# Edge tables copied in two halves, in pieces, inside the first pass of a graph network kernel

## The chip, the cores and the metric

The kernel runs on one core of a Trainium2 chip. The metric is device time in microseconds (us) of one execution; less is better. Five engines work beside each other, each with its own queue of instructions served in order: PE (matrix products), DVE (vector work), ACT (activation functions, and here a queue that issues DMA), POOL (here: indirect DMA, that is gathers and scatters), SP (here: a queue that issues DMA). Sixteen DMA engines move the data of all queues.

## What is computed

Four graph layers on one graph of N = 6250 nodes with D = 16 features and E = 200000 edges; after each the layer's result is added to x and normalized per node. The edges' inputs are `src`, `dst`, `edge_weight`, `edge_weight1` and `edge_attr_16`.

```python
edge_index = jnp.stack([src, dst])
x = _layernorm(x + _L0_gnn_ref(x, edge_weight, src, dst), axis=-1)        # segment_sum(tanh(x[src] * edge_weight), dst)
x = _layernorm(x + _L1_gnn_ref(x, edge_attr_16, W_msg, b_msg, W_attn, b_attn, src, dst), axis=-1)
x = _layernorm(x + _L2_gnn_ref(x, edge_weight1, W, b, src, dst), axis=-1)  # segment_max(x[src] * edge_weight1, dst) @ W.T + b
x = _layernorm(x + _L3_gnn_ref(x, edge_index, ...), axis=-1)               # two GIN convolutions with segment_sum(x[src], dst)
```

Layer 1 makes two 16 x 16 matrices per edge from its 16 features (`efeat @ W_msg + b_msg`, `efeat @ W_attn + b_attn`), multiplies both with the features of the source node, takes a softmax of the second over the edges of each target node and sums the first with it. The inputs given here have their edges sorted by `dst`.

## The kernel before

Edge p * 1600 + j lies in partition p (of 125) at column j (of J = 1600). The kernel needs edges in order of their targets.

**The start.** SP loads x, dst (`load_dst`) and src. DVE compares neighbouring targets (L274, L275), PE adds up the 125 partitions' answers, and `unordered` (L280) is the number of partitions in which an edge goes backwards, read into a register on every engine. DVE and PE then make the keys of the first 120 columns (`keys_first`, L265: `keys_made`, `keys_turned`, `keys_kept`), SP writes them to `key_d` (L252) and reads two blocks back, spread over 125 partitions (`load_keys`, L262, into `keys0`). ACT waits for the first of them (the copy to `arrived`, L285) and issues three copies from DRAM to DRAM (L287): edge weights to `ew_d` and `ew1_d` (0.8 MB each) and edge features to `ef_d` (12.8 MB). L289 is the branch around `sort_edges`: where `unordered` is above 0, the edges are sorted, and every input of the edges is scattered to its place (the list `given`, L199), over what the copies wrote. With the given inputs the branch is not taken; the engines meet at its end.

**The first pass** (`edge_scan("l0", ...)`) goes over eight batches of 200 columns. For 80 columns of each, POOL gathers the rows of x (L97, one gather a column, tile `xb`, two buffers). For the other 120, DVE makes one-hot matrices from a block of keys (`one_hot`, L469; SP asks for keys two blocks ahead), PE multiplies them with the table of x (L499, `select`), and DVE picks and sums (L503, L508). In the batch that follows, the message is formed (`tanh_message`: DVE times `ew` at L912, ACT's tanh at L914) and DVE scans it along the edges (L533). The order on each engine is that in which the program is written (`tc.manual_schedule`).

**Beside the first pass** runs a list of jobs (`prelude`): `at(k, ...)` puts a job before the k-th of 240 selects. Among them are the keys of later batches, the ends of the nodes' edges (51 gathers on POOL, `in_run`), the table of chunks for layer 1 (50 scatters on POOL, `chunk_d`), the load of `ew` from `ew_d` (k = 20), and `edge_rows`: 64 times 25 columns of `ef_d` are loaded by SP (`er_ef`, L681, by way of `store`, L93 and L94), split by ACT and DVE into three bf16 parts and written by SP to `edges_d`. The first of these loads is job 14.

**The later passes.** Layer 1 gathers chunks of `edges_d`, layer 2 repeats the scan with `ew1` (loaded at L1315 from `ew1_d`), layer 3 scans twice without weights.

Of the kernel before, what the change touches and what calls it, by code (L numbers as in the profile page):

```python
# [8 lines left out]
F32 = mybir.dt.float32  # L9
BF16 = mybir.dt.bfloat16  # L10
I32 = mybir.dt.int32
U16 = mybir.dt.uint16
# [8 lines left out]
P = 125  # L21
# [26 lines left out]
def tile_gnn_resnorm(ctx: ExitStack, tc: tile.TileContext, a: dict, out: bass.AP):  # L48
# [42 lines left out]
    def store(eng, to, of):  # L91

        eng.dma_start(to[:112], of[:112])  # L93
        eng.dma_start(to[112:], of[112:])  # L94
# [50 lines left out]


    src_d = dram.tile([E, 1], I32, name="src_d")
    dst_d = dram.tile([E, 1], I32, name="dst_d")
    ew_d = dram.tile([E, 1], F32, name="ew_d")
    ew1_d = dram.tile([E, 1], F32, name="ew1_d")  # L150
    ef_d = dram.tile([E, D], F32, name="ef_d")
    given = [(src_d, a["src"].unsqueeze(1)), (dst_d, a["dst"].unsqueeze(1)), (ew_d, a["edge_weight"].unsqueeze(1)),
# [4 lines left out]
    def sort_edges(sp, pp, dst):  # L157
# [6 lines left out]
        with tc.For_i(0, E, P) as e0:  # L164
# [33 lines left out]
            for t, (to, of) in zip(rows, given):  # L198
                nc.gpsimd.indirect_dma_start(  # L199
                    out=to, out_offset=bass.IndirectOffsetOnAxis(ap=at, axis=0), in_=t, in_offset=None)  # L200

# [55 lines left out]

    def load_keys(ep, k, keys=None):

        if keys is None:  # L260
            keys = ep.tile([P, BW], U16, name="keys", bufs=2)
        nc.sync.dma_start(keys, key_d[k * BC * P:k * BC * P + BW].partition_broadcast(P))  # L262
        return keys

    def keys_first(first):  # L265

        with tc.tile_pool(name="keys0p", bufs=1, space=PSUM) as pp:
            keys_kept(kp, 0, keys_turned(lambda r, c: pp.tile([128, 512], F32, name="scratch")[:r, :c], keys_made(kp, 0)))
        return [load_keys(kp, k, to) for k, to in enumerate(first)]

    with tc.tile_pool(name="sort", bufs=1) as sp, tc.tile_pool(name="sortp", bufs=1, space=PSUM) as pp:
        back = sp.tile([P, J], F32, name="backwards")
        worst = sp.tile([P, 1], F32, name="worst")
        nc.vector.tensor_tensor(back, dst[:, 1:J + 1], dst[:, :J], op=OP.is_lt)  # L274
        nc.vector.tensor_reduce(worst, back, AX.X, OP.max)  # L275
        n_ps = pp.tile([1, 1], F32, name="n_ps")
        nc.tensor.matmul(n_ps, worst, ones, start=True, stop=True)
        n_back = sp.tile([1, 1], I32, name="n_back")
        nc.vector.tensor_copy(n_back, n_ps)
        unordered = nc.values_load(n_back, min_val=0, max_val=P)  # L280
        keys0 = keys_first([None, None])
        arrived = consts.tile([1, 1], F32, name="arrived")
        with tc.manual_schedule():

            nc.scalar.copy(arrived, keys0[0][:1, :1])  # L285
            for to, of in given[2:]:
                nc.scalar.dma_start(to.rearrange("(p j) f -> p (j f)", p=1600),  # L287
                                    of.rearrange("(p j) f -> p (j f)", p=1600))
        with tc.If(unordered > 0):  # L289
            sort_edges(sp, pp, dst)  # L290
            nc.sync.dma_start(src, src_d.rearrange("(p j) o -> p (j o)", j=J))
            load_dst(dst, dst_d.rearrange("e o -> (e o)"))
            keys_first(keys0)

# [176 lines left out]

    def edge_scan(tag, table, parts, F, message, pen, tmp, beside=None, first=None, keys=None):

# [9 lines left out]
        with tc.tile_pool(name=f"es_{tag}", bufs=3) as ep, \  # L483
# [56 lines left out]

            keys = list(keys or [load_keys(ep, k) for k in range(0 if first is None else 1, 2)])
            ohs = one_hot(ep, keys.pop(0)) if first is None else first
# [135 lines left out]
    def edge_rows_load(e, c):  # L678
        if c < J:
            e.ef[c] = e.tmp.tile([P, WE, D], F32, name="er_ef", bufs=2)  # L680
            store(nc.sync, e.ef[c], ef_d.rearrange("(p j) f -> p j f", j=J)[:, c:c + WE, :])  # L681

# [233 lines left out]
    def prelude(kp):  # L916
# [6 lines left out]
        def at(k, do):  # L923
            jobs.setdefault(k, []).append(do)
# [13 lines left out]
        def put(**what):  # L938
            for k, f in what.items():
                now[k] = f  # L940
# [7 lines left out]
        for b in range(1, NB):  # L948
            k = 5 + 20 * (b - 1)
            at(k, lambda b=b: put(lo=keys_made(kp, b)))  # L950
            at(k + 3, lambda: put(kT=keys_turned(scratch, now["lo"])))
            at(k + 4, lambda b=b: keys_kept(kp, b, now["kT"]))
        at(12, lambda: put(e=ends_begin(now["sp"])))
        for i, j0 in enumerate(range(0, NJ1, NS)):
# [25 lines left out]
        for i in range(3):  # L980
            at(180 + 4 * i, lambda i=i: node_weights(i))
        at(20, lambda: store(nc.sync, ew, ew_d.rearrange("(p j) o -> p (j o)", j=J)))
        at(14, lambda: put(r=edge_rows_begin(now["rp"])))
# [8 lines left out]

    rows, carry = edge_scan("l0", a["x"], parts, D, tanh_message, None, lp0, prelude(kp), keys=keys0)
    x1 = node.tile([P, NJ, D], F32, name="x1")
# [316 lines left out]
    with tc.tile_pool(name="l2", bufs=1) as lp:  # L1311
        pen = lp.tile([P, J], F32, name="pen")
        nc.vector.tensor_scalar(pen, keep, -1.0, BIG, op0=OP.add, op1=OP.mult)
        ew1 = lp.tile([P, J], F32, name="ew1")
        nc.sync.dma_start(ew1, ew1_d.rearrange("(p j) o -> p (j o)", j=J))  # L1315

# [123 lines left out]
```

## Time and profile before

| | us |
|---|---|
| median of 3 runs | 7642.45 (7641.83 to 7643.04) |
| the profiled execution | 7640.91 |
| its span | 7639.1 |
| PE busy | 6793.4 (89%) |
| DVE busy | 6769.3 (89%) |
| POOL busy | 5894.5 (77%) |
| ACT busy | 1915.9 (25%) |
| first one-hot of the first pass (DVE L469) | starts at 74.77 |
| first gather of the first pass (POOL L97) | starts at 75.73 |
| first gather of layer 1 (POOL, tile `g`) | starts at 1279.74 |
| load of `ew1` for layer 2 (SP L1315) | issued at 4256.2 |

How to read it: times in the profile count from the start of the span. L12 is line 12 of the kernel before. Busy times of the engines overlap, so they don't add up to the span. A row names engine, line, operation, and the tile written <- the tiles read. What stands in brackets is the idle time of the engine ahead of the row and what ended it.

### The profile page before, as it was taken

To read this page: it belongs to the slowest core of one execution; us is meant where nothing else is said; L and a number is where in the kernel's file an instruction comes from. 1 tells how busy PE (TensorE), PEld (TensorE's weight loads), DVE (VectorE), ACT (ScalarE), POOL (GpSimd) and SP (SyncE) were. 2 spreads that over 40 slices of the span, in tenths; PEclk is the share of its full clock that TensorE was granted. 3 is DMA by queue.
4 is the path that set the end of the run, shared out by engine and by line. 5 is a ranking of instruction groups with operands and counts; after the bars stand their busy time and mean duration, and the time that the engine had idled before them with its cause. 6 is when DMAs were issued, how large, how long until landed. Compare 5 with 4: busy or idle time off the path is not lost. (4 is left out here: it accounts for less than half of the span.)

```text
span 7639.1 us, 133337 instructions
## 1 busy us (share of the span) xinstructions
PE 6793.4 (89%) x55586; PEld 5218.5 (68%) x55586; DVE 6769.3 (89%) x7933; ACT 1915.9 (25%) x3214; POOL 5894.5 (77%) x4906
## 2 busy tenths in 40 slices
PE   5888795799999999999999499999499998799995
PEld 5888795344444444444444299999499998799995
DVE  6999895899999999999999788999488887688885
ACT  0122120455555555555555400000000000000000
POOL 5888887777777777777777588888688887788886
PEclk9999897899999999999999799999699999899997
DMA  4344442122222222222222422222122222122221
GB/s 125 90 115 100 113 107 75 43 50 52 53 50 53 50 52 53 49 53 50 52 53 50 135 46 45 56 45 50 33 45 52 49 55 48 29 48 54 54 48 33
DMA packets 288155, 460.45 MB, mean 60 GB/s; under 512 B 135318, under 2 KB 187902, under 8 KB 283240
## 3 DMA queue, kind: packets, MB, share of 16 engines
q1 hardware_dynamic: 121160, 331.29, 12.9%
q0 software_dynamic: 166032, 106.01, 12.9%
q10 hardware_dynamic: 336, 14.40, 0.6%
q8 instruction: 442, 7.24, 0.4%
q14 instruction: 185, 1.52, 0.1%
HBM read 256.61 MB, written 206.15 MB: 61 GB/s over the span
## 5 line engine op out<-in xcount | busy, mean ns | idle before, releaser
L499 PE MATMUL all_ps<-parts,oh 125*128 125x208 bf16 (+1 forms) x46080 | 4004.1, 251 | 217.9 <-DVE kept L503 98.7
L499 PEld LDWEIGHTS <-oh 125*128 125x128 bf16 x46080 | 3985.5, 98 | 236.7 <-issue 130.1
L97 POOL DMA_INDIRECT hg<-table_x,g x1760 | 2061.5, 1171 | 545.1 <-issue 543.2
L97 POOL DMA_INDIRECT xb<-table_x,src x1280 | 1616.4, 1263 | 424.5 <-issue 423.6
L1101 PE MATMUL la<-e,ident 128*128 128x512 f32 x3520 | 1560.6, 596 | 4.5 <-DVE e L1088 3.8
L508 DVE TENSOR_REDUCE xb<-kept 125x64 f32<-125x832 f32 x960 | 1509.9, 1573 | 33.1
L503 DVE TENSOR_TENSOR kept<-all_ps,place 125x832 f32<-125x832 f32 x960 | 974.7, 1015 | 330.5 <-PE all_ps L499 322.6
L1101 PEld LDWEIGHTS la<-e,ident 128*128 128x128 f32 x3520 | 652.2, 190 | 743.9 <-issue 737.7
L97 POOL DMA_INDIRECT xb<-in_x,src x640 | 833.5, 1302 | 266.6 <-issue 193.3
L1053 DVE TENSOR_TENSOR e<-mm,hg 128x1024 f32<-128x1024 f32 x880 | 1013.4, 1210 | 10.6 <-DMA hg<-table_x,g 10.5
L97 POOL DMA_INDIRECT xb<-table_l3b,src x640 | 797.2, 1246 | 208.7 <-issue 208.7
L1048 PE MATMUL mm<-w_h,eT 98*128 98x512 bf16 x1760 | 668.1, 380 | 237.5 <-DVE e L1053 167.5
L469 DVE TENSOR_SCALAR oh<-keys,mykey 125x1504 bf16<-125x1504 uint16 x1272 | 792.8, 684 | 78.0 <-SPq L289 55.5
L1065 ACT ACTIVATE e<-e,epen 128x256 f32<-128x256 f32 x1760 | 797.6, 501 | 112.1 <-DVE e L1053 110.5
L1081 ACT ACTIVATE e<-e 128x1024 f32<-128x1024 f32 x440 | 465.1, 1057 | 1001.8 <-DVE e L1079 984.6
L1049 PE MATMUL mm<-w_l,eT 98*128 98x512 bf16 x1760 | 669.4, 380 | 0.0
L1049 PEld LDWEIGHTS <-eT 98*128 98x128 bf16 x1760 | 169.7, 96 | 637.5 <-issue 533.3
L1079 DVE TENSOR_TENSOR e<-e,st 128x1024 f32<-128x1024 f32 x440 | 519.4, 1221 | 7.6
L1088 DVE TENSOR_TENSOR e<-e 128x1024 f32<-128x1024 f32 x440 | 516.4, 1214 | 0.0
L1048 PEld LDWEIGHTS <-eT 98*128 98x128 bf16 x1760 | 170.8, 97 | 238.6 <-issue 57.1
L461 ACT ACTIVATE ln_s<-ln_s,eps_t 125x35 f32<-125x35 f32 (+1 forms) x8 | 2.5, 315 | 1176.2 <-DVE ln_s L460 1176.2
L97 POOL DMA_INDIRECT g<-edges_d,eidx x220 | 208.0, 946 | 83.7 <-PE la L1102 64.9
(366 smaller groups left out, 3457.4 us busy)
## 6 DMA issues: line engine op xcount, KB each, us to landing
keys<-key_d SPq DMA_DIRECT2D x318, 367.2 KB
rows_l<-st SPq DMA_DIRECT2D x220, 384.0 KB
edges_d<-er_t SPq DMA_DIRECT2D x64, 546.9 KB
hg<-table_x,g POOLq DMA_INDIRECT x1760, 2.6
rows_l<-sc SPq DMA_DIRECT2D x16, 1400.0 KB
xb<-table_x,src POOLq DMA_INDIRECT x1280, 2.8
ef_d<-in_edge_attr ACTq DMA_DIRECT2D x1, 12500.0 KB
er_ef<-ef_d SPq DMA_DIRECT2D x64, 175.0 KB
```

What stands on the lines that cost most here:

```text
L97: nc.gpsimd.indirect_dma_start(out=dst_ap, out_offset=None, in_=table, in_offset=bass.IndirectOffsetOnAxis(ap=idx, axis=0))
L469: nc.vector.tensor_scalar(oh[:, g, :], keys, mykey[:, g:g + 1], None, op0=OP.is_equal)
L499: nc.tensor.matmul(o, oh[:, g, (c + i) * P:(c + i) * P + 128], parts[:, q, a0:a0 + n, :].rearrange("p a f -> p (a f)"), start=(g == 0 and ...
L503: nc.vector.tensor_tensor(kept.rearrange("p (h i) a f -> p h (i a) f", i=2), all_ps[:P, :, :2 * W].rearrange("p h (i f) -> p h i f", f=F), ...
L508: nc.vector.tensor_reduce(xb[:, j:j + SG, :], kept.rearrange("p i a f -> p i f a"), AX.X, OP.add)
L1048: nc.tensor.matmul(ps[:, i, :], eT[:, s + i, :], w_h, start=True, stop=False)
L1049: nc.tensor.matmul(ps[:, i, :], eT[:, s + i, :], w_l, start=False, stop=True)
L1053: nc.vector.tensor_tensor(e[:, s:s + 2, :].rearrange("p s (i x) -> p (s i) x", x=2 * D), ps.rearrange("p s (i x) -> p (s i) x", x=2 * D), ...
L1065: nc.scalar.activation(part(e, 0)[:, k], part(e, 0)[:, k], AF.Identity, bias=epen[:, t, k:k + 1])
L1079: nc.vector.tensor_tensor(sc, sc, top.rearrange("p (i o) -> p i o", o=D).unsqueeze(1).to_broadcast([128, 4, D, D]), op=OP.subtract)
L1088: nc.vector.tensor_tensor(part(e, 1)[:, s:s + 4], part(e, 1)[:, s:s + 4], part(e, 0)[:, s:s + 4], op=OP.mult)
L1101: nc.tensor.matmul(ps, ident, e[:, s, :], start=(s == 0), stop=False)
```

## The change

The tables `ew_d`, `ew1_d` and `ef_d` get two halves of E rows. `sort_edges` scatters to the first; the inputs as they came are copied to the second. A new register `half` on SP holds E where no edge goes backwards and 0 otherwise, and every load from the three tables starts at that row (`by_target`). The copies are taken out of the place ahead of the branch and written as jobs 1 to 10 of the first pass: one each for the weights, eight for the features, of 25000 edges (1.6 MB) each, all issued by ACT. The copy to `arrived` is gone. Keys are no longer read ahead of the branch; `edge_scan` reads its first two blocks itself.

```diff
-    ew_d = dram.tile([E, 1], F32, name="ew_d")
-    ew1_d = dram.tile([E, 1], F32, name="ew1_d")
-    ef_d = dram.tile([E, D], F32, name="ef_d")
+    ew_d = dram.tile([2 * E, 1], F32, name="ew_d")
+    ew1_d = dram.tile([2 * E, 1], F32, name="ew1_d")
+    ef_d = dram.tile([2 * E, D], F32, name="ef_d")
...
-                    out=to, out_offset=bass.IndirectOffsetOnAxis(ap=at, axis=0), in_=t, in_offset=None)
+                    out=to[:E, :], out_offset=bass.IndirectOffsetOnAxis(ap=at, axis=0), in_=t, in_offset=None)
...
-    def load_keys(ep, k, keys=None):
-
-        if keys is None:
-            keys = ep.tile([P, BW], U16, name="keys", bufs=2)
+    def load_keys(ep, k):
+
+        keys = ep.tile([P, BW], U16, name="keys", bufs=2)
         nc.sync.dma_start(keys, key_d[k * BC * P:k * BC * P + BW].partition_broadcast(P))
         return keys
 
-    def keys_first(first):
-
+    def keys_first():
         with tc.tile_pool(name="keys0p", bufs=1, space=PSUM) as pp:
             keys_kept(kp, 0, keys_turned(lambda r, c: pp.tile([128, 512], F32, name="scratch")[:r, :c], keys_made(kp, 0)))
-        return [load_keys(kp, k, to) for k, to in enumerate(first)]
...
         unordered = nc.values_load(n_back, min_val=0, max_val=P)
-        keys0 = keys_first([None, None])
-        arrived = consts.tile([1, 1], F32, name="arrived")
-        with tc.manual_schedule():
-
-            nc.scalar.copy(arrived, keys0[0][:1, :1])
-            for to, of in given[2:]:
-                nc.scalar.dma_start(to.rearrange("(p j) f -> p (j f)", p=1600),
-                                    of.rearrange("(p j) f -> p (j f)", p=1600))
+        came = sp.tile([1, 1], I32, name="came")
+        nc.vector.tensor_scalar(came, n_ps, 0.0, float(E), op0=OP.is_equal, op1=OP.mult)
+        half = nc.values_load(came, engines=(mybir.EngineType.SP,), min_val=0, max_val=E)
+        keys_first()
         with tc.If(unordered > 0):
             sort_edges(sp, pp, dst)
             nc.sync.dma_start(src, src_d.rearrange("(p j) o -> p (j o)", j=J))
             load_dst(dst, dst_d.rearrange("e o -> (e o)"))
-            keys_first(keys0)
+            keys_first()
+
+    def by_target(t):
+        return t[bass.ds(half, E), :]
...
-            keys = list(keys or [load_keys(ep, k) for k in range(0 if first is None else 1, 2)])
+            keys = [load_keys(ep, k) for k in range(0 if first is None else 1, 2)]
...
-            store(nc.sync, e.ef[c], ef_d.rearrange("(p j) f -> p j f", j=J)[:, c:c + WE, :])
+            store(nc.sync, e.ef[c], by_target(ef_d).rearrange("(p j) f -> p j f", j=J)[:, c:c + WE, :])
...
+        for i, (to, of) in enumerate(given[2:4]):
+            at(1 + i, lambda to=to, of=of: nc.scalar.dma_start(to[E:, :].rearrange("(p j) o -> p (j o)", p=80),
+                                                               of.rearrange("(p j) o -> p (j o)", p=80)))
+        for i in range(8):
+            at(3 + i, lambda i=i: nc.scalar.dma_start(
+                ef_d[E + i * E // 8:E + (i + 1) * E // 8, :].rearrange("(p j) f -> p (j f)", p=100),
+                a["edge_attr_16"][i * E // 8:(i + 1) * E // 8, :].rearrange("(p j) f -> p (j f)", p=100)))
...
-        at(20, lambda: store(nc.sync, ew, ew_d.rearrange("(p j) o -> p (j o)", j=J)))
+        at(20, lambda: store(nc.sync, ew, by_target(ew_d).rearrange("(p j) o -> p (j o)", j=J)))
...
-    rows, carry = edge_scan("l0", a["x"], parts, D, tanh_message, None, lp0, prelude(kp), keys=keys0)
+    rows, carry = edge_scan("l0", a["x"], parts, D, tanh_message, None, lp0, prelude(kp))
...
-        nc.sync.dma_start(ew1, ew1_d.rearrange("(p j) o -> p (j o)", j=J))
+        nc.sync.dma_start(ew1, by_target(ew1_d).rearrange("(p j) o -> p (j o)", j=J))
```

In the order of instructions that the built program has on ACT, the copies of both weights and the first four pieces of the features stand ahead of the branch, and four pieces behind it; SP's way past the branch waits for all eight hardware DMA semaphores, as before.

More of the change, by code (lines that the diff above doesn't have):

```diff
@@ L470, in one_hot, with edge_scan @@
         return oh
-    def edge_scan(tag, table, parts, F, message, pen, tmp, beside=None, first=None, keys=None):
+    def edge_scan(tag, table, parts, F, message, pen, tmp, beside=None, first=None):
         is_max = pen is not None
```

## The prediction

> **What bounds the kernel now.** I read the page's slices first, since the change touches the start: is time lost there?
>
> ```profile
> span 7639.1 us, 133337 instructions
> ...
> DVE  6999895899999999999999788999488887688885
> ...
> POOL 5888887777777777777777588888688887788886
> ```
>
> The first slice of 191 us is busy to 5 or 6 tenths, the next ones to 8 or 9. The stretches of the start and the order of time say why:
>
> ```profile
> 10.00:20.00 10.00, 0.62 (x3) 0.26 (x3) 8.52 (x24) 0.00 (x0) 0.00 (x0) 1.00 0.02 5
> ...
> 30.00:70.00 40.00, 0.00 (x0) 0.00 (x0) 0.00 (x0) 0.00 (x0) 0.00 (x0) 1.00 0.98 322
> ```
>
> ```profile
> 19.32 0.37 SPq L252 DMA_DIRECT2D key_d<-kT  x1
> 21.72 53.84 SPq L262 DMA_DIRECT2D keys<-key_d  x3
> 27.68 0.19 ACT L285 CAST arrived<-keys 1x1 f32<-1x1 uint16 x1 [25.64 <-SPq L289]
> 27.69 1.23 ACTq L287 DMA_DIRECT2D ew_d<-in_edge_weight  x2
> 28.96 0.60 ACTq L287 DMA_DIRECT2D ef_d<-in_edge_attr  x1
> 74.77 4.62 DVE L469 TENSOR_SCALAR oh<-keys,mykey 125x1504 bf16<-125x1504 uint16 x8 [55.48 <-SPq L289]
> ...
> 75.73 1.56 POOL L97 DMA_INDIRECT xb<-in_x,src  x1 [71.83 <-SPq L289]
> ```
>
> From 30 to 70 us no engine works (the columns are PE, its weight loads, DVE, ACT, POOL, clock, DMA share, GB/s) and the DMA engines are 98% busy at 322 GB/s with the three copies of L287, 14.4 MB. Everything waits at L289, the branch around the sort. Its own row shows how:
>
> ```profile
> L289 SPq EVENT_SEMAPHORE  x8: 17/17/17, 23.5 to 74.6; - x8
> ```
>
> SP passes the branch by waiting for all eight hardware DMA semaphores, the copies' among them, and the last comes at 74.6. POOL starts 1.1 us behind it.
>
> What sets the end of the pass that follows (75 to 1279 us) I took from the waits of that stretch (total, times, longest) and the pass's last steps:
>
> ```profile
> POOL xb L97 <- issue: 193.3, 634, 0.3
> ...
> DVE xb L912 <- DMA xb<-in_x,src: 39.2, 2, 19.7
> ```
>
> ```profile
> 1239.78 0.96 DVE L912 TENSOR_TENSOR xb<-xb,ew 125x768 f32<-125x768 f32 x1
> ...
> 1264.67 1.49 DVE L912 TENSOR_TENSOR xb<-xb,ew 125x1280 f32<-125x1280 f32 x1 [19.54 <-DMA xb<-in_x,src]
> ...
> 1279.74 0.97 POOL L97 DMA_INDIRECT g<-edges_d,eidx  x1 [16.89 <-DVE carried L610]
> ```
>
> POOL never waits for anything but its own 0.3 us of issue: 640 gathers of x, 51 of runs and 50 scatters of chunks in one unbroken row, from 75.73 on. DVE twice stands still for them, 19.66 us at 855 to 874 and 19.54 us at the end. So the first pass is a gather chain of 1264.67 - 75.73 = 1188.9 us from POOL's start, and DVE has 39.2 us to spare. The three later passes start behind it and are not touched.
>
> **The change, part by part.** The sum is made against the profiled execution, 7640.9 us with 7639.1 of span; the median of the runs is 7642.45, 1.5 more.
>
> 1. *Where the copies go.* The diff writes them into the first pass, but nothing on ACT holds them there. In the order of instructions of the built program, six of ACT's ten copies (ew, ew1 and four of the eight ef pieces: 0.8 + 0.8 + 4 x 1.6 = 8.0 MB) stand ahead of the branch, at ACT's very start; four pieces (6.4 MB) follow it. SP still waits for all eight DMA semaphores at the branch. So the wait is not removed; it gets shorter and starts earlier.
>
> 2. *When the branch is passed.* Copies: 288 packets of 50 kB, 18 for each of the 16 DMA engines, took from 29.5 (1.8 us after the first issue) to 74.6, 2.51 us each. 8.0 MB are 10 for each: 25.1 us. They now share the engines with x, dst and src (2.0 MB): 125 rows each, whose packets took 0.178, 0.35 and 0.40 us, 116 us in all or 7.2 for each engine. First data at 2.4 (first issue at 0.76 as SP's today, plus 1.6). Earliest end 2.4 + 25.1 + 7.2 = 34.7. ACT's second, third and fourth piece wait for semaphores of earlier transfers (x, dst, the first piece), so I add 2 us for gaps: 36.7. The compute ahead of the branch must end by then too: src landed by 12.5, the keys' 6.8 us ended at 19.3, key_d was there at 21.7. If src is 10 us late behind copies, that ends at 32, still covered; if it comes with the last of the copies, key_d ends the wait (rival B). POOL starts 1.1 later: 37.8 instead of 75.73, **37.9 us earlier**. Bounds: a packet alone on an idle engine took 1.85 us, so 2.4 + 18.5 + 7.2 = 28.1 and POOL 46.5 earlier; with src last, 45 and 29.6 earlier.
>
> 3. *The last 6.4 MB beside the pass.* 8 packets for each engine, 8 x 2.51 = 20 us from the branch on. A gather of x lands 3.2 us after its issue and POOL issues one each 1.51 us with eight in flight, so it can take 12 us before POOL waits. Bounds: 0, as at 1282 to 1300, where 7.3 MB of zeros kept the DMA engines full at 399 GB/s and the gathers kept their 1.25 us step; and, were every gather held until the copies are done, 20 + 3 - 8 x 1.5 = 11 us. The zeros went in packets of 3008 bytes, these have 50 kB; the row is near in load, not in packet size. I take **3 us lost**.
>
> 4. *Keys.* keys0 was read ahead of the branch and is now read behind it: issue to arrival 5.8 us (21.72 to 27.5), up to 20 more beside the copies. DVE and PE thus start 6 to 26 us behind POOL instead of 1 ahead. Cost 0, hidden by DVE's 39.2 us of waiting for gathers. POOL depends on DVE with room enough: ck_at is written at 589.1 and used at 668.4, the scans that free a batch's buffer end at 1070 for gathers at 1133.8, the last group of five in run_i at 328.8 for gathers from about 401. The nearest room is 64 us. Beyond 39 us each us of lateness would cost one.
>
> 5. *Small things.* One DVE comparison (0.15 us, as L279) and one more register load on SP, ahead of 7 us of key work that is covered. One or two register instructions before each of the 131 loads through `half`: SP's 128 er_ef issues take 0.3 to 0.4 us each and SP is idle most of the time; keys are asked for two batches (29 us) ahead. ew1 is loaded at 4256 and used at 4513. The 1.28 us table load of ACT moves to the first er_t copy, where ACT waits anyway. Together 0.
>
> 6. *The new wait on SP.* The first er_ef load now waits for all ef pieces, with the next keys queued behind it. It stands 51 us after DVE's start (74.8 to 125.9); the copies end some 20 to 30 us after the branch. Cost 0.
>
> Sum: -37.9 + 3 = **-35 us**; profiled 7606, and with the 1.5 to the median **7607**.
>
> **Rivals.**
>
> *A, more gain.* The copies overlap with the inputs better than added times say, with packets at 1.85 us and no gather delayed: 7642.45 - 46.5 = 7596. For it: the inputs ran at 248 GB/s, below the copies' 322. Against: no stretch of the copies was faster than 344 GB/s.
>
> *B, the inputs wait in line.* src is issued behind 50 kB packets and arrives with the last of them at 34.7; then 6.8 us of keys, 2.4 for key_d and one for issue: branch at 45, POOL at 46, 29.6 us earlier, and gathers lose 3 to 8: 7616 to 7621. For it: where the copies met the second keys load (the trace's packet records, about 30 us), five engines began their first copy only once the keys' packets were through, served as they came. Against: at most half of the copies are issued before src is, since ACT waits for x, dst and its own first piece.
> By the Trainium skill, "DMA: Bandwidth & Descriptors", section "Queues, rings and completion order", a DMA engine takes turns between the queues that have work, a packet each: then src is not last, and the sum stays 7607, where service in order of arrival gives B's 7616 to 7621. In the few packets seen, the trace does not agree with it.
>
> *C, little or nothing.* B, and gathers held for the full 11 us, and the instruction fetches at the branch behind copies as well (PE's took 3.9 us on idle DMA engines; five times that is 16 more): gain 29.6 - 11 - 16 = 3, 7640.
>
> *D, slower.* Step 6 goes wrong: SP stands at er_ef, keys run out. It decides once copies last longer than 51 us, plus 29 of keys in hand, plus DVE's 39, plus the 35 won: 154 us after DVE's start, 6.4 MB at 42 GB/s. At 200 us: 7688. Against it: DMA engines 25% busy in that stretch and 322 GB/s before.
>
> **How the numbers follow.** Forecast 0.55 (7600 to 7614 by itself), A 0.12, B 0.20, C 0.08, D 0.05. The predicted time is 7607. The range 7596 to 7622 takes in the bounds of step 2, B, and leaves out C and D. About 0.2% (15 us, 7627) is what measuring can tell from no change: faster is forecast, A and B, 0.87; same is C, 0.08; slower D, 0.05.
>
> **What would show it.** Right: ACT's first DMA issue at about 0.8; SP's last wait at the branch at 35 to 38; POOL's first gather near 38; DVE's first one-hot 6 to 26 us later; then again an unbroken POOL row, the last gather's wait on DVE still there at the end, and g's first gather near 1245; the later passes as long as before. Wrong: a branch past 42 (B), gaps over 0.3 us between POOL's first 30 gathers (step 3), no wait of DVE for gathers at the pass's end (then DVE, not POOL, sets it and step 4 failed), or SP held at er_ef (D).

## The result and the profile after

The changed kernel takes 7593.25 us (median of 5 runs, 7588.63 to 7595.56) against 7642.45; the ratio is 0.9935, with a 95% interval of 0.9921 to 0.995. The profiled execution took 7588.63 us with a span of 7586.8, which is 52.3 less than before. The forecast was 35 less. Where the 52.3 us lie, from first instructions of the stages in both traces:

| stage | before | after | difference |
|---|---|---|---|
| to POOL's first gather | 75.73 | 36.25 | -39.5 |
| first pass, to the first gather of `g` | 1204.0 | 1203.9 | -0.1 |
| layer 1, to the gather of `fx` | 2976.7 | 2975.6 | -1.1 |
| tail of layer 1, from `fx` to the store of `table_x` | 84.2 | 73.8 | **-10.4** |
| layer 2, from there to DVE's step on `carried` | 1048.3 | 1046.7 | -1.6 |
| layer 3 to the end | 2250.1 | 2250.6 | +0.5 |

First the page's slices after:

```profile
span 7586.8 us, 133608 instructions
...
DVE  7999994999999999999999789998589897688985
...
POOL 6888886777777777777777588888688887788886
```

DVE's first slice rose from 6 tenths to 7 and POOL's from 5 to 6; the rest can't be told apart at this scale. The stretch in which no engine worked (columns as before: PE, its weight loads, DVE, ACT, POOL, clock, DMA share, GB/s) now has work:

```profile
10.00:20.00 10.00, 0.00 (x0) 0.00 (x0) 0.42 (x2) 0.00 (x0) 0.00 (x0) 1.00 0.94 301
...
30.00:70.00 40.00, 13.40 (x125) 11.98 (x126) 13.67 (x17) 0.00 (x0) 25.89 (x21) 1.00 0.68 209
```

The copies moved from 30 to 70 us forward to the very start: 10 to 20 us, where the DMA engines had been 2% busy, is now at 94%. The order of time, and the branch's own row:

```profile
21.01 0.31 SPq L94 DMA_DIRECT2D src<-in_src  x1
...
21.47 1.82 DVE L272 TENSOR_TENSOR backwards<-dst 125x1600 f32<-125x1600 int32 x1 [11.05 <-DMA dst<-in_dst]
...
32.36 0.37 SPq L253 DMA_DIRECT2D key_d<-kT  x1
35.90 23.07 SPq L262 DMA_DIRECT2D keys<-key_d  x3
36.25 1.39 POOL L97 DMA_INDIRECT xb<-in_x,src  x1 [32.36 <-PEq L283]
...
56.31 5.11 DVE L466 TENSOR_SCALAR oh<-keys,mykey 125x1504 bf16<-125x1504 uint16 x8 [23.98 <-DMA xb<-in_x,src]
```

```profile
L283 SPq EVENT_SEMAPHORE  x8: 17/17/17, 33.3 to 35.2; - x8
```

SP's last wait at the branch fell from 74.6 to 35.2. What ended it is not what the forecast had at the end: by the trace's packet records the 8.0 MB of copies ahead of the branch were through at 33.1, while the store of `key_d` was only issued at 32.36 (before: 19.32) and SP's last wait ended 2.8 us behind that. The keys were late because dst was: DVE's comparison starts at 21.47, behind 11.05 us of waiting for dst, where it had started at 8.43. That is 13.0 us later, and `key_d` is 13.0 us later too. By the packet records the last row of dst came at 20.45 instead of 7.7, that of src at 23.17 instead of 10.7. The rest of src (L94) was also issued late, since SP stood still for dst ahead of it (total, times, longest):

```profile
SPq L94 <- DMA dst<-in_dst: 14.2, 1, 14.2
```

This cost nothing more, since src was there when DVE came to it at 25.57. The waits of the pass and its last steps:

```profile
POOL xb L97 <- issue: 193.0, 633, 0.3
...
DVE xb L909 <- DMA xb<-in_x,src: 18.3, 2, 16.4
```

```profile
1240.19 0.97 POOL L97 DMA_INDIRECT g<-edges_d,eidx  x1 [16.82 <-DVE carried L607]
```

POOL's row is unbroken but for two gathers (idle 1.24 and 1.13 us at 51 and 53, waiting for earlier gathers), DVE's waiting for gathers shrank from 39.2 to 18.3 us, and the gathers still end the pass.

**The tail of layer 1** was in no step of the forecast. First before, then after, in order of time (POOL's gather of `fx`, SP's loads, ACT's and DVE's steps; the tile `ew` of these rows is `ew1`, digits are left out):

```profile
4256.22 0.71 SPq L1315 DMA_DIRECT2D ew<-ew_d  x1
4256.41 0.94 POOL L97 DMA_INDIRECT fx<-rows_l,fix_row  x1 [31.95 <-PE own_ps L1244]
...
4278.73 1.28 ACT L1258 ACT_TABLE_LOAD   x1 [12.79 <-DMA r<-rows_l,idx_row]
...
4282.61 0.31 ACT L1201 ACTIVATE now<-now 128x128 f32<-128x128 f32 x1
...
4285.90 0.42 DVE L1222 TENSOR_TENSOR fx_top<-l_carry,fx 128x256 f32<-128x256 f32 x1
```

```profile
4215.82 0.94 POOL L97 DMA_INDIRECT fx<-rows_l,fix_row  x1 [31.70 <-PE own_ps L1248]
...
4223.27 0.30 SPq L1319 DMA_DIRECT2D ew<-ew_d  x1
4225.46 0.31 ACT L1205 ACTIVATE now<-now 128x128 f32<-128x128 f32 x1 [5.36 <-DVE now L1204]
...
4227.56 1.28 ACT L1262 ACT_TABLE_LOAD   x1 [1.53 <-DMA r<-rows_l,idx_row]
...
4228.39 0.42 DVE L1226 TENSOR_TENSOR fx_top<-l_carry,fx 128x256 f32<-128x256 f32 x1
```

Before, the load of `ew1` (0.8 MB) starts together with the gather of `fx`, and the gathers of `r` behind it land late: ACT's logarithm of `r` (the table load ahead of it is the row shown) starts 22.3 us behind `fx`. On ACT the second half's exponential (`now`) stands behind it, so `fx_top` comes 29.5 us behind `fx`. After, the load starts 7.5 us, the logarithm 11.7 us and `fx_top` 12.6 us behind `fx`. The change of the diff there is only the row at which the load of `ew1` starts. What differs is the order of SP and ACT and the place of tiles. What holds SP there in the changed kernel (the waits of SP's queue in that stretch: total, times, longest):

```profile
SPq L1319 <- DVE flat L1191: 9.1, 1, 9.1
```

`ew1` now waits for DVE to be done with the tile `flat`; before, the load followed that of the keys at once. The first keys and one-hot of layer 2 have moved too, from behind layer 1 (4255.66 and 4261.81) to ahead of it (1314.67 and 1319.40). The two tiles of keys0 are gone from the pool they were in (2 x 3008 bytes of each partition), and pools, tiles and orders that are worked out from free memory came out another way 4000 us later.

### The profile page after: what moved, and what is told of

Same layout as the page of the kernel before. It is cut to its first block, busy times and chain, and to the rows that moved or that the text cites. A ratio compares the mean times of both kernels' runs of the same rounds, so it can differ in the third digit from the quotient of the medians.

```text
span 7586.8 us, 133608 instructions
## 1 busy us (share of the span) xinstructions
PE 6793.3 (90%) x55586; PEld 5221.5 (69%) x55586; DVE 6766.1 (89%) x7934; ACT 1909.6 (25%) x3213; POOL 5888.9 (78%) x4906
## 5 line engine op out<-in xcount | busy, mean ns | idle before, releaser
L496 PE MATMUL all_ps<-parts,oh 125*128 125x208 bf16 (+1 forms) x46080 | 4007.3, 251 | 172.3 <-DVE kept L500 76.2
L496 PEld LDWEIGHTS <-oh 125*128 125x128 bf16 x46080 | 3988.3, 99 | 191.3 <-issue 107.4
L505 DVE TENSOR_REDUCE xb<-kept 125x64 f32<-125x832 f32 x960 | 1509.3, 1572 | 33.1
```

The costliest lines, as they stand in the source:

```text
L496: nc.tensor.matmul(o, oh[:, g, (c + i) * P:(c + i) * P + 128], parts[:, q, a0:a0 + n, :].rearrange("p a f -> p (a f)"), start=(g == 0 and ...
L505: nc.vector.tensor_reduce(xb[:, j:j + SG, :], kept.rearrange("p i a f -> p i f a"), AX.X, OP.add)
```

## The experiments

The kernel before took 7.64 to 8.19 ms in different sets of runs (the extra time lies in the long passes), so a time is compared only within its set, by its ratio to the kernel before there; stages come from one profile of each. The times of the result above are the first measurement, and sets 1 to 5 came behind it; set 1 has no run of the changed kernel, and m1, which differs from it in two tiles alone, stands in for it there.

| kernel | ratio, 95% interval | POOL's first gather | first `g` | `fx` to `table_x` |
|---|---|---|---|---|
| before, first measurement | 1 | 75.7 | 1279.7 | 84.2 |
| changed, first measurement | 0.9935, 0.9921 to 0.995 | 36.3 | 1240.2 | 73.8 |
| m1 (set 1) | 0.9952, 0.9929 to 0.9975 | 36.3 | 1247.0 | 84.3 |
| k1 (set 1) | 0.999, 0.9973 to 1.0008 | 67.5 | 1273.1 | 76.2 |
| n1 (set 1) | 0.9934, 0.9912 to 0.9955 | 22.9 | 1231.8 | 74.0 |
| h1 (set 1) | 0.9959, 0.9941 to 0.9976 | 22.8 | 1244.6 | 78.4 |
| a1, changed (set 2) | 0.9957, 0.9941 to 0.9973 | 35.8 | 1304.6 | 73.5 |
| p1 (set 2) | 0.9971, 0.9956 to 0.9986 | 23.0 | 1309.6 | 73.7 |
| t1 (set 2) | 0.9988, 0.9976 to 1.0 | 75.2 | 1339.8 | 73.7 |
| c2 (set 2) | 0.9973, 0.9958 to 0.9987 | 61.3 | 1330.8 | 74.6 |
| b1, before (set 3) | 0.9996, 0.9985 to 1.0007 | 74.9 | 1278.7 | 83.9 |
| a2, changed (set 3) | 0.9948, 0.9935 to 0.9961 | 36.0 | 1245.3 | 72.4 |
| u1 (set 3) | 0.9934, 0.9921 to 0.9947 | 35.6 | 1250.0 | 72.7 |
| p2 (set 3) | 0.994, 0.9928 to 0.9952 | 22.5 | 1239.1 | 73.6 |
| a3, changed (set 4) | 0.9956, 0.9939 to 0.9974 | 35.7 | 1305.6 | 73.1 |
| u2 (set 4) | 0.9969, 0.9952 to 0.9986 | 36.5 | 1324.5 | 74.2 |
| p3 (set 4) | 0.9924, 0.9907 to 0.9942 | 22.9 | 1311.3 | 72.3 |
| a4, changed (set 5) | 0.9943, 0.993 to 0.9956 | 36.5 | 1247.9 | 72.2 |
| p3 again (set 5) | 0.9918, 0.9903 to 0.9932 | 22.5 | 1235.9 | 72.1 |

Up to POOL's first gather, and from `fx` to `table_x`, before in set 3 and changed in sets 2 to 5 repeat the first numbers to within 1 and 2 us. A single stage from `fx` to `table_x` can still lie off: h1 has the changed kernel's order and load there and took 78.4 us, with 4.35 us of waiting in POOL's gathers of `r` where the changed kernel has 1.16.

### Was it the freed memory? m1 and k1

m1 is the changed kernel with two tiles of the old size taken again:

```diff
+        for i in range(2):
+            spare = kp.tile([P, BW], U16, name=f"spare{i}")
+            nc.vector.memset(spare[:1, :2], 0)
```

> The changed kernel with the SBUF of the two early key tiles (2 x 3008 bytes a partition, in the pool of the keys) taken again by two tiles that nothing uses; in its order of instructions layer 2's first keys load and one-hot stand behind layer 1 again, as in the kernel before. Theory: some 10 of the 49 us come from layer 1's end, because the freed memory let that load and one-hot move ahead of layer 1. Expected: start as in the changed kernel (POOL's first gather near 36), fx gather to table store 84 us as in the kernel before, 7603. Rival (that gain comes from the tables' new places or ew1's load through a register): stays at 7593.

k1 is the kernel before with the keys part of the change alone; the copies stay as they were, but ACT waits for `place1` in place of the keys:

```diff
-        keys0 = keys_first([None, None])
+        keys_first(None)
...
-            nc.scalar.copy(arrived, keys0[0][:1, :1])
+            nc.scalar.copy(arrived, place1[:1, 0, 0, :1])
...
-    rows, carry = edge_scan("l0", a["x"], parts, D, tanh_message, None, lp0, prelude(kp), keys=keys0)
+    rows, carry = edge_scan("l0", a["x"], parts, D, tanh_message, None, lp0, prelude(kp))
```

> The kernel before with the keys part of the change alone: the first two key blocks are read in the scan, behind the branch; the three copies stand ahead of the branch as before, held by the key work (place1) instead of by the first keys. Theory: layer 1's end is 10 us shorter through the freed memory, and the copies start 6 to 8 us earlier (about 20 instead of 27.7), so POOL starts near 69 and the time is 7642 - 10 - 7 = 7625. Rival (the gain at layer 1's end belongs to the tables in two halves): 7635.

ACT's steps at the tail of layer 1 in m1:

```profile
4310.78 1.28 ACT L1265 ACT_TABLE_LOAD   x1 [13.05 <-DMA r<-rows_l,idx_row]
...
4314.66 0.31 ACT L1208 ACTIVATE now<-now 128x128 f32<-128x128 f32 x1
```

The logarithm is late again (21.9 us behind the gather of `fx` at 4288.84) and the exponential behind it; the load of `ew1` starts together with that gather again (4288.81). With the memory taken the stage is 84.3 us, with the keys part of the change alone 76.2. So the 10 us come from the freed memory, and not from the copies or the register. The stages of m1 came out as forecast, those of k1 nearly (POOL from 67.5 for 69, 8 us off the tail for 10); the interval of m1's ratio takes in its rival's time too (7593, 0.9935), and k1's ratio can't be told from 1 and is that of its rival (7635). k1's profile has the start 8.2 us earlier, since ACT no longer waits for the keys to be read back.

### Which of the two that moved: the load or ACT's order? t1, u1, u2, b1

My theory was ACT's order: the exponential behind the logarithm. t1 is the kernel before with the load of `ew1` alone moved, into layer 2's pass.

```diff
-        nc.sync.dma_start(ew1, ew1_d.rearrange("(p j) o -> p (j o)", j=J))
...
-        rows, carry = edge_scan("l2", t2, parts, D, scaled_message, pen, lp, first=first)
+        rows, carry = edge_scan("l2", t2, parts, D, scaled_message, pen, lp,
+                                {12: [lambda: nc.sync.dma_start(ew1, ew1_d.rearrange("(p j) o -> p (j o)", j=J))]}, first)
```

> The kernel before with one line moved: ew1's load stands in layer 2's pass instead of at the tail of layer 1; ACT's order at that tail stays that of before. Theory (ACT's order makes the 10 us): fx to table_x stays at 82 to 85 us, time within 3 us of the kernel before. Rival (ew1's 0.8 MB load, issued together with the gathers of fx, holds up the gathers of r): fx to table_x falls to 74 to 78 and the time by 6 to 10 us.

```profile
4456.67 1.28 ACT L1258 ACT_TABLE_LOAD   x1 [2.71 <-DMA r<-rows_l,idx_row]
...
4460.55 0.31 ACT L1201 ACTIVATE now<-now 128x128 f32<-128x128 f32 x1
```

The theory fell. ACT's order is that of before (logarithm, then exponential), and the stage takes 73.7 us: the logarithm starts 11.5 us behind the gather of `fx` (4445.22). Moving one load is enough. The exponential behind the logarithm costs nothing by itself: `fx_top` comes 18.6 us behind `fx` here and 12.6 in the changed kernel, in stages of the same length. b1 is the kernel before once more, as the control for this:

> The kernel before itself, for its stages on the chip of this call, whatever the speed of its long passes: POOL's first gather near 75.5, and 84 us from the first gather of fx to the store of table_x, as on the first chip, if those 84 us belong to the kernel and not to the chip.

It has 83.9. The other direction, the changed kernel with a load put where `ew1`'s was: u1 copies 0.8 MB of rows_l from DRAM to DRAM, u2 loads 0.64 MB of it into SBUF. Neither is read by anything.

```diff
+    spare = dram.tile([128, 2 * RW], F32, name="spare")
+    nc.sync.dma_start(spare.rearrange("p (t c) -> p t c", t=2), rows1_v[:, QS - 2:QS, :])
```

> The changed kernel with one load more: at the end of layer 1, SP copies 0.8 MB of rows_l in 128 packets of 6 kB into a tensor that nobody reads, issued together with the gather of fx, where the kernel before issued ew1; orders of all engines else unchanged. If the load beside the gathers of r is what cost 10 us (as the run with ew1's load moved says), fx to table_x grows from 73.8 to 80 to 86 us, and the time by 6 to 12 us. If ACT's order of the exponentials and the logarithm of r is what mattered, it stays at 73 to 76, since that order is the changed kernel's.

```diff
+    nc.sync.dma_start(parts_all[:P].bitcast(F32)[:, :1272],
+                      rows1.rearrange("(p t) c -> p (t c)", t=Q)[:P, (QS - 2) * RW:(QS - 2) * RW + 1272])
```

> The changed kernel with one load more: at the end of layer 1, SP loads 0.64 MB of rows_l (125 rows of 5 kB) into the table parts, which the next layer's split overwrites, together with the gather of fx, as the kernel before did with ew1; orders of all engines else unchanged, ACT's with the exponentials first. If a load into SBUF beside the gathers of r is what cost the 10 us, whatever ACT's order, the first logarithm of r starts 18 to 22 us behind fx's gather instead of 11.7, and fx to table_x grows from 73 to 79 to 84 us. If ACT's order protects the chain, fx to table_x stays at 73 to 76 though the logarithm is late. If the logarithm is not late either, then the load's bytes are not what delayed the gathers, and that stays open.

u1 was a miss: its copy started 2.0 us ahead of `fx`, delayed the logarithm by less than 1 us (12.6 behind `fx`) and cost nothing. u2's load started 1.7 us ahead of `fx` and delayed the logarithm by 4.8 us:

```profile
4418.41 0.31 ACT L1207 ACTIVATE now<-now 128x128 f32<-128x128 f32 x1 [5.36 <-DVE was L1202]
...
4425.28 1.28 ACT L1264 ACT_TABLE_LOAD   x1 [6.30 <-DMA r<-rows_l,idx_row]
```

The logarithm is 16.5 us behind `fx` (4408.77), the exponential is not held, and the stage takes 74.2 us, 1 more than the changed kernel of its set. So with the exponential ahead of the logarithm a lateness of 4.8 us cost 1 us, no more than these stages scatter by. Taking the load away is enough by itself. Whether the order alone would cover the full lateness of 10.6 us isn't shown, since neither stand-in made `r` that late. The packet records say why they did not: `ew1`'s packets in the kernel before passed between 4.6 and 19.8 us behind the gather of `fx`, beside the gathers of `r`, but u1's were through 2.1 us and u2's 7.5 us behind it.

### What the copies cost at the start: n1, h1, c2

n1 leaves the copies out and reads the inputs' own tables, so it holds for sorted edges alone:

```diff
-        for i, (to, of) in enumerate(given[2:4]):
...
-            store(nc.sync, e.ef[c], by_target(ef_d).rearrange("(p j) f -> p j f", j=J)[:, c:c + WE, :])
+            store(nc.sync, e.ef[c], a["edge_attr_16"].rearrange("(p j) f -> p j f", j=J)[:, c:c + WE, :])
...
-        at(20, lambda: store(nc.sync, ew, by_target(ew_d).rearrange("(p j) o -> p (j o)", j=J)))
+        at(20, lambda: store(nc.sync, ew, a["edge_weight"].rearrange("(p j) -> p j", j=J)))
...
-        nc.sync.dma_start(ew1, by_target(ew1_d).rearrange("(p j) o -> p (j o)", j=J))
+        nc.sync.dma_start(ew1, a["edge_weight1"].rearrange("(p j) o -> p (j o)", j=J))
```

> The changed kernel without any copies: features and weights are read from the inputs themselves, so the part that serves unsorted edges is left out; sorted edges give the same output. Theory: the copies are all that holds the branch beyond 23.5, so POOL starts near 25 (11 us earlier than with the change) and loses nothing to copies (2 us): 7580, and that is what copies still cost. Rival (the gathers' start is not what sets the pass): 7593.

h1 keeps all copies behind the branch (ACT waits for the tile `keep`, which the first pass makes):

```diff
+    arrived = consts.tile([1, 1], F32, name="arrived")
...
+        at(1, lambda: nc.scalar.copy(arrived, keep[:1, :1]))
```

> The changed kernel with all ten copies held behind the branch: ACT first copies one element of a tile that DVE writes at job 1 of the scan. Theory: branch passed at 23.5, POOL from 25, DVE from about 31; 14.4 MB beside the pass for 45 us cost the gathers 2 to 5 us where 6.4 MB cost 2: 7584. Rival (gathers and keys held by 50 kB packets in line, up to 11 us for each 20 us of copies, and er_ef's wait at select 14 stalls the keys): 7600 or more.

Without copies POOL starts at 22.9: 13.3 us of the changed kernel's 36.3 are the copies'. The first `g` of n1 comes 15.2 us earlier than in m1 of the same set, so the gathers' start does set the end of the pass. The time doesn't decide: the interval of n1's ratio takes in the theory's 7580 (0.992) and the rival's 7593 (0.9935).

Held back, the copies cost as much again, as the rival of h1 had it: h1 starts at 22.8 too, but its gathers wait ten times for DMA (total, times, longest):

```profile
POOL xb L97 <- DMA xb<-in_x,src: 17.1, 10, 3.5
```

Of the 17.1 us 14.1 are over their usual 0.3 each, and the first `g` comes only 2.4 us earlier than in m1. My estimate for step 3 was thus right only for few bytes at a time. In the changed kernel 4.8 MB of the 6.4 went from 34.9 to 52.3 us, the last 1.6 alone from 60.2 on, and the gathers lost 1.8 us. In h1 14.4 MB went from 42.5 to 96.9 us with one gap of 1.8 us, and cost 1 us for each MB.

c2 asks what makes dst late. It is the changed kernel with `ef_d` copied by one instruction, so that 14.4 MB stand ahead of the branch:

```diff
-        for i in range(8):
-            at(3 + i, lambda i=i: nc.scalar.dma_start(
...
+        at(3, lambda: nc.scalar.dma_start(ef_d[E:, :].rearrange("(p j) f -> p (j f)", p=1600),
+                                          a["edge_attr_16"].rearrange("(p j) f -> p (j f)", p=1600)))
```

> The changed kernel with ef copied by one instruction instead of eight: all 14.4 MB stand ahead of the branch. By the packet price of step 2 (2.51 us for each of 18 packets an engine, from 2.4) the copies end at 48 to 52, some 15 us later than in the changed kernel, and no gather of the pass waits for them (1.8 us won). If engines take turns between the queues, dst and src arrive as in the changed kernel (near 21 and 25), key_d is stored by 33, and the branch is passed when the copies end, at 50 to 53: 14 to 16 us slower than the changed kernel. If packets are served in the order they came, dst waits for all of the copies, src for them too, and the keys follow at 60 to 66: 25 to 30 us slower.

The DMA queues of c2 between 12 and 42 us (queue: packets, MB, share of 16 engines; q10 is ACT's, q1 SP's), then what DVE waited for:

```profile
q10 hardware_dynamic: 187, 9.35, 89.5%
q1 hardware_dynamic: 188, 1.02, 12.2%
```

```profile
DVE backwards L272 <- DMA dst<-in_dst: 30.0, 1, 30.0
```

Packet for packet, 187 against 188: the engines take turns between the two queues. By the Trainium skill, "DMA: Bandwidth & Descriptors", section "Queues, rings and completion order", a DMA engine goes round the queues that have work for it, a packet at a time. The trace agrees in the turns, one record of the profile for each. That such a packet is typically 9 to 17 descriptors, as the section adds, doesn't show here: the 123 middle rows of dst, some 8 for each engine, did not pass in one turn but between 6.9 and 27.4 us.

What both theories of the expectation had wrong is what follows from the turns. A packet of the copies has 50 kB, one of SP's queue 5.4 on average, and a turn takes 2.6 us (30 us for 188 packets on 16 engines); x, dst and src have 125 rows each, some 8 turns on each engine. So DVE could use dst only at 40.17 and src at 51.17, `key_d` was stored from 57.99 on and POOL began at 61.3, 25 us behind the changed kernel. The copies themselves were through at 50.3. The 25 us are the number of the theory of service in order, but its reason is not there. In the changed kernel ACT's queue had only 4.8 MB by then and ran dry at 19.4 us; the last row of dst came at 20.45. Turns keep the last byte from waiting for all copies, but they give the large packets nine parts of ten.

### Can the 13 us be had? p1, p2, p3

Three ways to place the copies so that they meet neither the inputs nor many gathers. p1: ACT waits for `keep`, then copies pieces by columns, each shortly ahead of its readers, 24 selects apart.

```diff
+        at(1, lambda: nc.scalar.copy(arrived, keep[:1, :1]))
+        for k, (to, of) in zip((2, 22), given[2:4]):
...
+            at(24 * i + 10 if i else 3, lambda i=i: nc.scalar.dma_start(
+                ef_d[E:, :].rearrange("(p j) f -> p j f", j=J)[:, i * J // 8:(i + 1) * J // 8, :],
...
```

> The copies in step with their readers: ACT waits for keep ahead of the first copy, ef goes in eight pieces by columns (200 of each partition's 1600 rows), piece i about 24 i selects into the pass, just ahead of the loads that read it. My theory: 36.2 - 22.9 = 13.3 us of the start belong to copies ahead of the branch, and held copies cost 14 us of gathers only because 14.4 MB come at once; in pieces of 1.6 MB with 150 us between them a gather's eight in flight cover each piece (the changed kernel lost 1.8 us to four pieces). POOL's first gather at 23 to 24, gathers' waits on DMA below 3 us, first gather of g 11 to 14 us earlier than in the changed kernel of this call. Rival: SP stands at er_ef behind each piece, the next keys are late, DVE loses more than its 18 us and g's first gather comes no earlier. Other rival: packets delay gathers whenever they come, 1 us and more for each of the nine, and 9 to 14 us are given back.

p2: the weights once src is there (ahead of the branch), the features in two bursts of four pieces.

```diff
+            nc.scalar.copy(arrived[:, :1], src[:1, :1])
...
+        at(1, lambda: nc.scalar.copy(arrived[:, 1:], keep[:1, :1]))
+        at(6, lambda: nc.scalar.copy(arrived[:, 1:], now["lo"][:1, :1]))
...
+            at(3 if i < 4 else 7, lambda i=i: nc.scalar.dma_start(
...
```

> The changed kernel with its copies placed by data: ew and ew1 once src has landed (near 12.5, 1.6 MB while the keys are made), four pieces of ef once keep is there (behind the branch), four more once select 5 has made its keys. Theory: each burst of 6.4 MB costs gathers about 2 us (the changed kernel lost 1.8 to its one burst), dst and src wait for no copy, so POOL's first gather comes near 23 to 24 instead of 36 and 4 us are given back: the first gather of g 8 to 11 us earlier than in the changed kernel, time 0.10 to 0.14% below it where gathers set the end of the pass. Rival: as in the run with all copies held, whatever comes behind the branch is paid in full (1 us per MB), and g's first gather comes within 3 us of the changed kernel's. Other rival: er_ef's first load waits for the second burst, and DVE loses more than its room.

p3: the weights as in p2, the eight pieces one at a time, every fourth select, by a mark that DVE sets; the rows of `edges_d` begin 24 selects later, so that no load meets a copy under way.

```diff
+        def piece(i):
+            nc.vector.memset(ticks[:, i:i + 1], 0.0)
+            nc.scalar.copy(ticks[:, 14:15], ticks[:, i:i + 1])
+            nc.scalar.dma_start(
...
+        for i in range(8):
+            at(1 + 4 * i, lambda i=i: piece(i))
...
-        at(14, lambda: put(r=edge_rows_begin(now["rp"])))
+        at(38, lambda: put(r=edge_rows_begin(now["rp"])))
...
-                at(19 + 3 * i + step, lambda i=i, step=step: edge_rows(now["r"], i * WE, step))
+                at(43 + 3 * i + step, lambda i=i, step=step: edge_rows(now["r"], i * WE, step))
```

> The changed kernel with its copies spread: ew and ew1 once src has landed, and the eight pieces of ef one at a time, every fourth select (some 16 us apart) by a small DVE mark that ACT waits for; the rows of edges_d begin 24 selects later, so that no load of er_ef waits for a piece. Theory: a single piece of 1.6 MB (two packets for each DMA engine, 5 us) is covered by the eight gathers in flight, so gathers lose below 3 us where bursts of four lost 10: POOL's first gather at 22.5 to 24, the first gather of g 9 to 12 us earlier than in the changed kernel, time 0.12 to 0.16% lower. Rival: copies cost the gathers about 0.8 us for each MB wherever they stand (14.1 us for 14.4 MB held, 10.3 for 12.8 in two bursts, 13 ahead of the branch), and g's first gather comes within 4 us of the changed kernel's.

> The kernel with the spread copies once more. If the pass ends with the gathers on this chip (g's first gather waits 17 us for DVE as in the first profile), the first gather of g comes 9 to 13 us earlier than in the changed kernel of this call and the ratio lies 0.0012 to 0.0030 below its. If PE sets the pass here too (wait of 70 us), the stage is no earlier or later by more than a few us, and only the ratio of the times can tell. Rival: no difference in the ratio, and the 0.9924 of the last call was scatter.

The changed kernel ran in each set as the yardstick:

> The changed kernel itself on the chip and in the hours of the other runs, as their yardstick. Expected: POOL's first gather near 36, first gather of g near 1240 to 1245, 73.8 us between the first gather of fx and the store of table_x, and a time 0.55 to 0.75% below the kernel before of this chip, as the first measurement. If the kernel with the freed memory held (ratio 0.9952) were only scatter between chips, this run would stand at 0.995 as well.

> The changed kernel on the chip of this call: POOL's first gather near 36, first gather of g 35 to 40 us earlier than in the kernel before, fx to table_x 73 to 75 us. Yardstick for the paced version.

> The changed kernel on the chip of this call, as yardstick: POOL's first gather near 36, fx to table_x 72 to 74 us.

> The changed kernel as yardstick for the spread copies: POOL's first gather near 36, waits of gathers for DMA 2 to 3 us in all, ratio to the kernel before 0.9935 to 0.9957 as in the other calls.

p1 lost no gather to a copy and was no faster: SP stood still at the loads of `er_ef` six times for pieces under way, 97.4 us in all, and DVE waited 30.8 us at the splits of `er_ef` (8.3 in a1). Its set couldn't show a gain at `g` either way: POOL waited there at the end of the pass for DVE, 76.7 us in p1 and 72.8 in a1, against 16.8 in the first measurement, so the gathers didn't set its end. p2's bursts cost the gathers 10.3 us (12.4 less seven times 0.3), so the first `g` comes 6.2 us earlier than in a2, and the ratios overlap. The bursts were hardly apart: 8.0 MB went from 41.4 to 70.4 us and 4.8 from 72.1 to 89.3, much like h1's.

p3 works where the gathers set the end of the pass. The waits of POOL's gathers over the first pass, in a4 and in p3 of the same set:

```profile
POOL xb L97 <- DMA keys<-key_d: 32.6, 1, 32.6
...
POOL xb L97 <- DMA xb<-in_x,src: 2.5, 5, 1.1
```

```profile
POOL xb L97 <- SPq L289: 18.6, 1, 18.6
...
POOL xb L97 <- DMA xb<-in_x,src: 0.3, 1, 0.3
```

The long wait at the start is 14 us shorter and no gather waits for a copy: the first `g` comes at 1235.9 instead of 1247.9. The ratio is 0.9918 (0.9903 to 0.9932) against 0.9943 (0.993 to 0.9956) there, and 0.9924 (0.9907 to 0.9942) against 0.9956 (0.9939 to 0.9974) in set 4. p3 is clearly faster than the kernel before. Against the changed kernel it is 0.25% and 0.32% lower; in each set the two intervals overlap at their ends, and it is the two sets together that speak for it. The forecast was 0.12 to 0.16%; the 12 us at `g` are 0.16%, and what more there may be has no cause shown. In set 4 the profile doesn't show the cause: `g` comes 5.7 us later than in a3 (whose profiled run was the fastest of its ten, 8072 against a median of 8159), and POOL waited 73.2 us for DVE at the end of the pass, so that the gathers no longer set its end.

## Why the prediction was right and wrong

- **Step 1, where the copies go:** right. ACT's first copy is issued at 0.76, six copies ahead of the branch, four pieces behind it.
- **Step 2, when the branch is passed:** 36.7 forecast, 35.2 measured; POOL 37.8 and 36.25. That this fits is in part luck. The copies were through at 33.1, before both the sum's 34.7 and the 36.7 with gaps, and they did not end the wait: "If src is 10 us late behind copies, that ends at 32, still covered" was the right path with too small a lateness. Both dst and src came 12 to 13 us late, dst held the keys, and these were 13.0 us late: 21.7 and 13.0 make 34.7, behind the copies. The two paths lie so close that the number hides the mistake.
- **Step 3, 3 us lost beside the pass:** 1.8 (1.24 and 1.13, less the usual 0.3 each), inside its bounds.
- **Step 4, keys:** right. DVE starts 20 us behind POOL and its waiting for gathers shrinks from 39.2 to 18.3.
- **Step 5, small things:** the register and the loads cost nothing that can be seen. It has no term for the two tiles that are gone.
- **Step 6:** right; SP is not held at er_ef.
- **The step that failed:** "The three later passes start behind it and are not touched." The prediction has no number behind it: orders were compared near the edit only. The two tiles of keys0 that are gone moved layer 2's first one-hot, ACT's order and the load of `ew1`; the last put 10.4 us less between `fx` and `table_x` (m1 for the memory, t1 for the load). The other misses are 4.6 us in the start and the first pass (39.6 for 35: POOL began 1.6 earlier than forecast, and the pass from there was no longer than before, where 3 had been added) and 2.2 in layers 1 to 3. Without the 10.4 us the time would have lain inside the range.
- **Rivals:** the measured time lies below A's 7596, but A's reason was not there: the packets ahead of the branch took 2.28 us on average, not 1.85. Against A stood that no stretch of the copies was faster than 344 GB/s; that depends on the stretch, for the profile before has 337 from 30 to 40 us and 400 from 31 to 33. B's reason was there in part: inputs do wait, by turns and not in line, and c2 shows its price once the copies are longer. The sentence that with turns src is not last and the sum stays came out in its number only: the keys behind dst ended the wait, and in c2 the sum doesn't hold. That the engines do take turns, which the few packets seen before the result seemed to contradict, c2's trace shows. C and D did not occur.

## What to carry to other kernels

A freed or added tile is an edit to the whole program: compare the order of instructions and the waits of every queue to the end, not only around the diff. Where all work waits at one point, place large copies so that they meet neither the loads that feed the way to that point nor a row of gathers, or in pieces small and far enough apart that the transfers in flight cover each (here 1.6 MB, 14 us and more apart). A load of no urgency beside gathers that something waits for is worth moving.

## What the runs showed of the hardware

- Turns between two DMA queues go by packets, not by bytes: in c2 187 packets of 50 kB against 188 of 5.4 kB on average in 30 us, 9.35 MB against 1.02.
- The copies cost 13.3 us of POOL's start with 8.0 MB ahead of the branch and 38.4 with 14.4 MB (c2 against n1). Beside gathers, 14.4 MB in two long stretches cost 14.1 us (h1), 12.8 MB in two cost 10.3 (p2), and pieces of 1.6 MB issued 14 to 26 us apart nothing that can be seen (p3 in set 5).
- In sets 2 and 4 PE stood still more often with nothing shown that it waited for: in a1 its weight loads of the scans sat idle 731.1 us in all against 191.3 in the changed kernel's first profile, at nearly the same granted clock (0.955 and 0.959), and the kernel took 8.1 ms. The chip of set 2 took 7.7 ms in set 3. The cause is open.
